# Layer 0's sorted sums with one plain and two weighted spline blocks a direction, the plain blocks copied by ScalarE

## The chip, the cores and the metric

One core of a Trainium2 chip runs the whole program. The metric is the device time of one execution in microseconds (us); the number that counts is the median over several executions. The engines are TensorE (PE, with its weight loads as PEld), VectorE (DVE), ScalarE (ACT), GpSimd (POOL) and SyncE (SP, which only issues DMAs here). Each runs its own instructions in order, and they wait for each other by semaphores.

## The reference

Two layers of a graph network run over 12,500 nodes of 32 features and 400,000 edges, which come sorted by destination. Layer 0 is a spline convolution: every edge has two coordinates in [0, 1]; each gives three hat functions, their products are nine weights, and the message is the source's row times a mix of nine 32 x 32 matrices. Messages are summed by destination, divided by the degree, and a root product, a bias, a residual and a layer norm follow. Layer 1 is relational: four basis matrices, weighted by the edge's type.

```python
p = jnp.clip(pseudo, 0.0, 1.0)
grid = jnp.linspace(0.0, 1.0, KSIZE, dtype=p.dtype)          # KSIZE = 3
dist = jnp.abs(p[:, :, None] - grid[None, None, :])
b = jnp.maximum(1.0 - dist * (KSIZE - 1), 0.0)
basis = jnp.einsum('ea,eb->eab', b[:, 0], b[:, 1])           # then nine in a row
...
messages = jnp.einsum('ek,ei,kio->eo', basis, x[row], weight)
out = jnp.zeros((x.shape[0], weight.shape[2]), dtype=x.dtype).at[col].add(messages)
...
out = out / jnp.maximum(degree, 1.0)[:, None]
out = out + x @ root_w.T + root_b
...
x = _layernorm(x + _L0_gnn_ref(x, edge_attr_2, L0_gnn_weight, L0_gnn_root_w, L0_gnn_root_b, edge_index), axis=-1)
x = _layernorm(x + _L1_gnn_ref(x, L1_gnn_W, L1_gnn_edge_type_weight, src, dst, edge_type_8), axis=-1)
```

For a coordinate in [0, 1] the three hat functions add up to 1. The change uses this.

## The kernel before

The program has three stages: a sorting stage, layer 0 and layer 1. The edges are cut in two parts. The first part (groups 0 to 31 of layer 0's numbering, in blocks of 56 tiles of 128 edges) is the "near" path: its source rows are fetched from memory by POOL, one gather for 128 rows (`gather`, L125), and summed per node (class `Near`, L866 to 1122). The other 90 groups (32 to 121, 2304 edges each) are sorted by source in the first stage, so that their rows can be made on the chip from one-hot products.

For each sorted group, layer 0 does the following (function `layer`, L1145). `take` reads the group's slots (`sl`, L1281) and VectorE makes one-hots from them (`s`, L1293). PE multiplies them with the node rows into one of three PSUM banks (L1303, seven products a bank), and ScalarE moves each bank to its place in `yt` (L1310, 14 moves a group). `use` then goes through the group in three pieces of six chunks of 128 edges. For a piece, PE turns `yt` back into rows `y` in PSUM (L1323, two buffers in one bank). VectorE does three things: `hot_b`, the one-hot of the destination within the group (L1335, 82 places, bf16); `outer`, the rows times the second direction's three spline values (L576, called at L1342, 6 x 3 x 32 = 576 elements); and `spread`, the first direction's three values times the one-hot (L1343, 6 x 3 x 82 = 1476 elements). PE then sums, for each chunk, `outer` (97 columns: three blocks of 32 and a one for the degree) against `spread` (246 columns) into `agg` in PSUM (L1356), over the group's 18 chunks.

The sum of a piece is issued one piece late (`LAG` is 1). `outer` has three buffers (`products`), `spread` three, `hot_b` two. The first direction's spline values `b0_ps` lie in the same PSUM bank as `agg` (L1179): ScalarE writes them once a group (`first_spline`, L1209), and the spread reads them there. The other spline values are made by ScalarE for five groups at a time (`splines`, L1194: six Abs, one Relu).

At a group's end ScalarE copies the sum out of PSUM (`weighing`, L589), and PE multiplies its three blocks, one for each first-direction value, by the matrices in `w0_sb` (L595). `w0_sb` is loaded once, at the start (L203 to 206); its last row holds ones in the degree's column. Work of the near path, of finished nodes (`fin`) and of layer 1's preparation (`mixed`) is put between the pieces. The frame orders instructions by the time it expects them to be ready; in some places the text holds one behind another (`issue_after`).

The last part of the program (from L1489) is a loop over all edges that runs only if the sorting found the data unfit, and it uses `w0_sb` too (L1524).

Of the kernel before, what the change touches and what calls it, by code (L numbers as in the profile page):

```python
# [17 lines left out]
P = 128  # L18
# [4 lines left out]
def kernel(  # L23
# [76 lines left out]
    assert NBL * B == NW  # L100
    assert 8 * NG <= GE // 2 and 1024 <= GE and PER * E == P * N and NGS * CHS * P == E and T1 > 0 and NS * SUB == CH
    assert DUMMY >= N and NG <= P and NTAB // P % 9 == 0 and NCO * CO * CH <= GE
    assert WB * JQ == BT and MAXR % 2 == 0 and 2 * SUB * D + MAXR <= 4 * P and KJ * MAXR + 6 * CH <= 4 * P and NB0 * BT * P <= E and RR <= P
    assert WB * D == P and NTAB >= NW * P and W1 == P
    SRC_UNIT = P * NR
    assert N * SRC_UNIT < 1 << 24
# [95 lines left out]
    nc.sync.dma_start(xr[:TAIL, NW - 1, :], x[(NW - 1) * P:, :])  # L202
    w0_sb = const.tile([P, KJ, D + 1], F32)  # L203
    nc.gpsimd.memset(w0_sb, 0.0)
    nc.vector.memset(w0_sb[KR:KR + 1, :, D:], 1.0)
    nc.sync.dma_start(w0_sb[:KR, :, :D], w0.rearrange("k i o -> (k i) o").rearrange("(j r) o -> r j o", r=KR))
    w1_sb = const.tile([W1, D], F32)
    nc.sync.dma_start(w1_sb, w1.rearrange("b i o -> (b i) o"))
    etw_sb = const.tile([P, NB, NR], F32)
# [362 lines left out]
            nc.vector.memset(t[:, :, W0:], 1.0)  # L572
        return out_

    def outer(t, co, xg, c, k):
        return nc.vector.tensor_tensor(  # L576
            t[:, :c, :k * D].rearrange("p c (k d) -> p c k d", k=k),
            co[:, :, :, None].to_broadcast([P, c, k, D]),
            xg[:, :, None, :].to_broadcast([P, c, k, D]), op=ALU.mult)

# [564 lines left out]
    def layer(which):  # L1145
# [5 lines left out]
        with ExitStack() as stack:  # L1151
# [24 lines left out]
            ys = y_bank[:, :2 * SUB * D].rearrange("p (i c d) -> p i c d", i=2, c=SUB)  # L1176
            sum_bank = ps.tile([P, 4 * P], F32, name="agg")
            if which == 0:
                b0_ps = sum_bank[:, KJ * MAXR:KJ * MAXR + 6 * CH].rearrange(  # L1179
                    "p (i k c) -> p i k c", i=2, k=3)  # L1180
            else:
                col_ps = y_bank[:, 2 * SUB * D:2 * SUB * D + MAXR]
                nc.vector.tensor_copy(col_ps, col[:, :MAXR])
# [10 lines left out]
            def splines(g0):  # L1194
                if g0 <= GF:
                    load_args(g0)
                load_args(g0 + CO)
                args_s = loaded.pop(0)
                b = [cos1.tile([P, 3, CH, CO], F32, name=f"co_b{i}", bufs=2) for i in range(2)]
                for i in range(2):  # L1200
                    for k in range(3):
                        nc.scalar.activation(b[i][:, k], args_s[:, i], AF.Abs,
                                             bias=knot[:, k:k + 1])
                nc.scalar.activation(b[1], b[1], AF.Relu, bias=1.0, scale=-2.0)
                for i in range(CO):
                    co_of[g0 + i] = [t[:, :, :, i] for t in b]
# [107 lines left out]
            def use(g, yt):  # L1314
# [3 lines left out]
                def product(s):  # L1318
                    along(g, s)
                    y = ys[:, (g * NS + s) % 2]  # L1320
                    for c in range(SUB):
                        k = s * SUB + c
                        nc.tensor.matmul(y[:, c, :], yt[:M3, k * P:(k + 1) * P],  # L1323
                                         add3[:M3, :], start=True, stop=True)
                    cs = slice(s * SUB, (s + 1) * SUB)
                    rel = rel_s[:, cs, g, None, :]
                    t = products[(g * NS + s) % NOUT]
                    if which == 0:
                        hot = prods.tile([P, SUB, MAXR], BF16, name="hot_b", bufs=2)
                        spread = prods.tile([P, SUB, 3, MAXR], F32, name="hot")  # L1330
                        b0, b1 = [v[:, cs] for v in co_of[g]]
                    else:
                        hot = spread = prods.tile([P, SUB, MAXR], F32, name="hot")
                    hots[s] = spread
                    nc.vector.tensor_tensor(  # L1335
                        hot.rearrange("p c (m i) -> p c m i", i=2),
                        rel.to_broadcast([P, SUB, MAXR // 2, 2]),
                        (col_ps if which else col_b)[:, None, :]
                        .rearrange("p c (m i) -> p c m i", i=2)
                        .to_broadcast([P, SUB, MAXR // 2, 2]), op=ALU.is_equal)  # L1340
                    if which == 0:
                        last[0] = outer(t, b1, y, SUB, 3)  # L1342
                        nc.vector.tensor_tensor(  # L1343
                            spread, b0[:, :, :, None].to_broadcast([P, SUB, 3, MAXR]),
                            hot[:, :, None, :].to_broadcast([P, SUB, 3, MAXR]), op=ALU.mult)
                    else:
                        last[0] = outer(t, co_of[g][:, cs, :], y, SUB, NB)

# [156 lines left out]
    def weighing_(layer, agg, r):  # L1505
# [15 lines left out]
        def apply():  # L1521
            po = at[0][:, KJ * P:KJ * P + D]
            for j in range(kj):
                nc.tensor.matmul(po, at[1][:, j, :], w1_sb if layer else w0_sb[:KR, j, :D],  # L1524
                                 start=(j == 0), stop=(j == kj - 1))
            nc.scalar.activation(r[:, :D], po, AF.Copy)
            if layer == 0:
# [56 lines left out]
    def from_table(q, tab, width):  # L1584
# [4 lines left out]
                          tab[q0 * P:(q0 + w) * P, :].rearrange("(w p) d -> p w d", p=P))  # L1589
        return t  # L1590

    count = nc.values_load(again[0:1, 0:1], min_val=0, max_val=1)
    with tc.For_i(0, count, 1) as _:
        for t, a, inner in ((src_a, src, 1), (dst_a, dst, 1), (typ_a, edge_type, 1),
                            (attr_a, edge_attr, 2)):
            nc.sync.dma_start(t.rearrange("p (g c) -> p g c", c=CHS * inner),
# [45 lines left out]
```

## Time and profile before

| | |
|---|---|
| median of 6 executions | 6240.28 us (6217.77 to 6282.72) |
| the profiled execution | 6295.12 us, span 6293.3 us |
| mean granted TensorE clock | 0.725 |
| busy over the span | PE 54%, PEld 46%, DVE 48%, ACT 30%, POOL 39% |
| sorting stage | 0 to about 960 us |
| layer 0's sorted groups | about 960 to 3640 us |
| layer 1 | about 3640 to 6293 us |
| DVE spread L1343 | 270 x 1693 ns = 457.2 us |
| DVE outer L576, layer 0 | 270 x 751 ns = 202.7 us |
| DVE hot_b L1335, layer 0 | 270 x 406 ns = 109.7 us |
| PE agg L1356, layer 0 | 3240 records, 847.6 us |
| ACT yt L1310, both layers | 2968 x 384 ns = 1141.0 us |
| POOL gathers of layer 0 L125 | 1505 x 1008 ns |

Busy time is the time in which an engine has an instruction running, whatever it waits for before. "Remote", or an unknown queue, stands where the profile can't tell who ended a wait, and "issue" where the engine waited for nothing that the profile shows. A matmul in f32 appears as two records. Times in this text count from the span's start.

### The profile page before, as it was taken

Reading aid. Unit: us, or ns where it says so; the run is one execution under the profiler, and the core shown is the slowest. Engines: PE = TensorE matmul, PEld = TensorE weight load, DVE = VectorE, ACT = ScalarE, POOL = GpSimd, SP = SyncE. Lnnn points to the kernel's source line nnn. Section 1 sums busy time; section 2 is a strip of 40 time slices with the busy share of each in tenths; the row PEclk is TensorE's granted clock in tenths of the full one; section 3 lists DMA queues with packets and bytes.
Section 4 is the critical chain, followed back from the end, with each engine's and each line's share of the span. In section 5 each row is a group of like instructions: output and inputs, shape, how many; then the busy total and the mean of one; then the engine's idle time right before and its main releaser. Section 6 shows DMA issues by size and latency. Waiting matters only on the chain.

```text
span 6293.3 us, 111686 instructions
## 1 busy us (share of the span) xinstructions
PE 3425.0 (54%) x40923; PEld 2910.0 (46%) x40923; DVE 3046.2 (48%) x5178; ACT 1918.1 (30%) x4768; POOL 2440.5 (39%) x2486
## 2 busy tenths in 40 slices
PE   0221126566556665566556847656555565655558
PEld 0110114455444444455445636555544555555558
DVE  3785776455445554455445625334333334333336
ACT  2664643222222222222222314222222222222224
POOL 5475653333433334433443131333344333334330
PEclk9855557777777777777767868767776677677768
DMA  3000014223222322223222324333333333333333
GB/s 60 8 14 11 13 37 122 84 89 95 80 81 86 95 86 79 86 81 101 81 78 84 117 79 157 110 107 118 111 103 101 103 112 117 108 111 103 104 101 119
DMA packets 266348, 555.44 MB, mean 88 GB/s; under 512 B 84944, under 2 KB 152560, under 8 KB 265300
## 3 DMA queue, kind: packets, MB, share of 16 engines
q1 hardware_dynamic: 184672, 500.96, 24.6%
q0 software_dynamic: 78768, 41.81, 4.9%
q8 instruction: 321, 5.26, 0.3%
q10 hardware_dynamic: 2348, 5.45, 0.3%
q14 instruction: 239, 1.96, 0.1%
HBM read 522.22 MB, written 25.76 MB: 87 GB/s over the span
## 4 chain that ended last, share of the span: by engine, by line
PE 42%; another core or an unknown queue 26%; issue 13%; DVE 11%; ACT 4%; DMA 1%; POOL 1%; ACTq 1%; SPq 0%; DVEq 0%
PE agg L1356 20%; PE bank L1303 13%; PE n_sum L732 3%; PE y L1323 2%; ACT yt L1310 2%; PE n_bank L1052 2%; DVE outer L576 1%; DVE hot L1343 1%; DVE args L387 1%; PE wg L1078 1%; DVE args L386 1%; PE wg L853 1%; PE wg L595 1%; DVE above L379 1%
## 5 line engine op out<-in xcount | busy, mean ns | idle before, releaser
L125 POOL DMA_INDIRECT n_xg<-in_x_dram,n_idx x1505 | 1516.4, 1008 | 1784.5 <-issue 438.5
L1303 PE MATMUL bank<-s,x 128*128 128x108 bf16 (+3 forms) x20776 | 1324.2, 212 | 1410.5 <-issue 962.4
L1310 ACT ACTIVATE yt<-bank x2968 | 1141.0, 384 | 2591.7 <-remote 1273.7
L1303 PEld LDWEIGHTS <-x 128*128 128x128 bf16 x20776 | 1085.7, 105 | 1557.9 <-issue 1489.3
L1356 PE MATMUL agg<-hot,outer 128*128 128x82 f32 (+1 forms) x7632 | 1548.5, 351 | 270.7 <-issue 181.4
L125 POOL DMA_INDIRECT n_xg<-z_dram,near_i x929 | 892.7, 961 | 1723.9 <-PE n_bank L1052 764.5
L1356 PEld LDWEIGHTS agg<-hot,outer 128*128 128x128 f32 (+1 forms) x7632 | 1188.9, 203 | 483.8 <-issue 242.8
L1293 DVE TENSOR_SCALAR s<-sl,row 128x1824 bf16<-128x1824 int16 x848 | 652.6, 772 | 855.4 <-remote 422.9
L1343 DVE TENSOR_TENSOR hot<-agg,hot_b 128x1476 f32<-128x1476 f32 x270 | 457.2, 1693 | 426.7 <-ACT agg_sb L589 134.4
L1335 DVE TENSOR_TENSOR hot<-in_order,y 128x492 f32<-128x492 bf16 x366 | 243.4, 665 | 666.2 <-remote 484.3
L576 DVE TENSOR_TENSOR outer<-co_b,y 128x576 f32<-128x576 f32 x270 | 202.7, 751 | 509.3 <-remote 283.8
L576 DVE TENSOR_TENSOR outer<-co,y 128x768 f32<-128x768 f32 x366 | 346.6, 947 | 0.0
L1323 PE MATMUL y<-add,yt 96*128 96x32 bf16 x3816 | 243.7, 181 | 129.9 <-issue 60.4
L1323 PEld LDWEIGHTS <-yt 96*128 96x128 bf16 x3816 | 203.6, 103 | 158.9 <-issue 152.2
L1052 PE MATMUL n_bank<-n_w,n_xg 128*32 128x72 f32 x3024 | 118.0, 269 | 244.7 <-issue 113.1
L589 ACT ACTIVATE agg_sb<-agg 128x82 f32<-128x82 f32 (+1 forms) x212 | 63.2, 298 | 502.8 <-PE agg L1356 240.2
L237 ACT ACTIVATE in_order<-src,thr 122x2304 bf16<-122x2304 int16 x97 | 213.9, 2205 | 0.5
L1052 PEld LDWEIGHTS n_bank<-n_w,n_xg 128*32 128x32 f32 x3024 | 72.8, 128 | 280.6 <-DVE n_w L1036 117.9
L732 PE MATMUL n_sum<-rows,n_hit 82*128 82x32 f32 (+1 forms) x1056 | 172.6, 287 | 39.3 <-issue 37.9
L732 PE MATMUL n_sum<-n_r,n_hit 112*128 112x33 f32 (+1 forms) x670 | 121.0, 313 | 112.3 <-issue 52.9
L729 DVE TENSOR_SCALAR n_hit<-cols,place_of 82x256 f32<-82x256 f32 (+2 forms) x294 | 94.7, 333 | 171.3 <-remote 68.5
L732 PEld LDWEIGHTS n_sum<-rows,n_hit 82*128 82x128 f32 x1056 | 155.1, 210 | 44.4 <-issue 40.8
(257 smaller groups left out, 2888.1 us busy)
## 6 DMA issues: line engine op xcount, KB each, us to landing
sl<-slots SPq DMA_DIRECT2D x424, 608.0 KB
sl<-slots SPq DMA_DIRECT2D x424, 456.0 KB
n_xg<-in_x_dram,n_idx POOLq DMA_INDIRECT x1505
n_xg<-z_dram,near_i POOLq DMA_INDIRECT x929
hd<-begin_d SPq DMA_DIRECT2D x848, 0.0 KB
z_dram<-n_z SPq DMA_DIRECT2D x49, 256.0 KB
co_d<-co SPq DMA_DIRECT2D x13, 360.0 KB
co<-co_d SPq DMA_DIRECT2D x13, 360.0 KB
```

What stands on the lines that cost most here:

```text
L125: return nc.gpsimd.indirect_dma_start(out=xg, out_offset=None, in_=table, in_offset=bass.IndirectOffsetOnAxis(ap=idx, axis=0))
L237: nc.scalar.activation(t, of[:NG], AF.Sign, bias=bias, scale=scale, accum_out=total)
L576: return nc.vector.tensor_tensor(t[:, :c, :k * D].rearrange("p c (k d) -> p c k d", k=k), co[:, :, :, None].to_broadcast([P, c, k, D]), xg ...
L732: nc.tensor.matmul(total[:, w % WB, :width], hit[:m, i * P:(i + 1) * P], r[:m, :width], start=fresh and i == 0, stop=final and i == len(ws ...
L1052: nc.tensor.matmul(o, self.xg[i][:, at[0], at[1], :], v, start=True, stop=True, tile_position=(0, j * D))
L1293: nc.vector.tensor_scalar(s[:, :n], sl[:, :n], row, None, op0=ALU.is_equal)
L1303: nc.tensor.matmul(bank[:, AHEAD + a:AHEAD + b], parts[:, w * M3:w * M3 + P], s[:, off_[j]:off_[j + 1]], start=(j == 0), stop=(j == B - 1) ...
L1310: moves.append(nc.scalar.activation(yt[:M3, ds(to, LONG)], bank[:M3, ds(place, LONG)], AF.Copy))
L1323: nc.tensor.matmul(y[:, c, :], yt[:M3, k * P:(k + 1) * P], add3[:M3, :], start=True, stop=True)
L1335: nc.vector.tensor_tensor(hot.rearrange("p c (m i) -> p c m i", i=2), rel.to_broadcast([P, SUB, MAXR // 2, 2]), (col_ps if which else col_ ...
L1343: nc.vector.tensor_tensor(spread, b0[:, :, :, None].to_broadcast([P, SUB, 3, MAXR]), hot[:, :, None, :].to_broadcast([P, SUB, 3, MAXR]), o ...
L1356: near.behind = nc.tensor.matmul(agg[0], t[:, c, :], v, start=(k == 0), stop=(k == CH - 1)).ins
```

## The change

The first hat function of each direction is written as one minus the other two. Then the sum over k of b_k W_k becomes W_0 + b_1 (W_1 - W_0) + b_2 (W_2 - W_0), in each direction. So the first of the three blocks of `outer` is the plain rows `y`, and the first of the three blocks of `spread` is the plain one-hot; ScalarE copies both. VectorE multiplies only the other two blocks of each (384 and 984 elements). The splines are made for two values instead of three. The differences of the matrices are taken once, at the start, in `w0_sb`: two more loads of parts of w0 go to `w0_z`, and VectorE subtracts. The degree's one stands in the first block's row alone. The fallback loop keeps the old form, so it gets its own unchanged copy of the matrices (`w0_l`), loaded inside the loop. `agg` keeps its shape.

```diff
--- before.py
+++ after.py
@@ -100,7 +100,7 @@
     assert NBL * B == NW
     assert 8 * NG <= GE // 2 and 1024 <= GE and PER * E == P * N and NGS * CHS * P == E and T1 > 0 and NS * SUB == CH
     assert DUMMY >= N and NG <= P and NTAB // P % 9 == 0 and NCO * CO * CH <= GE
-    assert WB * JQ == BT and MAXR % 2 == 0 and 2 * SUB * D + MAXR <= 4 * P and KJ * MAXR + 6 * CH <= 4 * P and NB0 * BT * P <= E and RR <= P
+    assert WB * JQ == BT and MAXR % 2 == 0 and 2 * SUB * D + MAXR <= 4 * P and KJ * MAXR + 4 * CH <= 4 * P and NB0 * BT * P <= E and RR <= P
     assert WB * D == P and NTAB >= NW * P and W1 == P
     SRC_UNIT = P * NR
     assert N * SRC_UNIT < 1 << 24
@@ -202,8 +202,17 @@
     nc.sync.dma_start(xr[:TAIL, NW - 1, :], x[(NW - 1) * P:, :])
     w0_sb = const.tile([P, KJ, D + 1], F32)
     nc.gpsimd.memset(w0_sb, 0.0)
-    nc.vector.memset(w0_sb[KR:KR + 1, :, D:], 1.0)
+    nc.vector.memset(w0_sb[KR:KR + 1, 0, D:], 1.0)
     nc.sync.dma_start(w0_sb[:KR, :, :D], w0.rearrange("k i o -> (k i) o").rearrange("(j r) o -> r j o", r=KR))
+    w0_z = work.tile([P, P], F32, name="n_xT")[:KR, :KJ * D].rearrange("p (j o) -> p j o", j=KJ)
+    nc.vector.memset(w0_z, 0.0)
+    for k in range(1, 3):
+        nc.sync.dma_start(w0_z[k * D:(k + 1) * D],
+                          w0.rearrange("(j k) i o -> k i j o", k=3)[0])
+    nc.vector.tensor_tensor(w0_sb[:KR, :, :D], w0_sb[:KR, :, :D], w0_z, op=ALU.subtract)
+    for j in range(1, KJ):
+        nc.vector.tensor_tensor(w0_sb[:KR, j, :D], w0_sb[:KR, j, :D], w0_sb[:KR, 0, :D],
+                                op=ALU.subtract)
     w1_sb = const.tile([W1, D], F32)
     nc.sync.dma_start(w1_sb, w1.rearrange("b i o -> (b i) o"))
     etw_sb = const.tile([P, NB, NR], F32)
@@ -572,9 +581,9 @@
             nc.vector.memset(t[:, :, W0:], 1.0)
         return out_
 
-    def outer(t, co, xg, c, k):
+    def outer(t, co, xg, c, k, at=0):
         return nc.vector.tensor_tensor(
-            t[:, :c, :k * D].rearrange("p c (k d) -> p c k d", k=k),
+            t[:, :c, at:at + k * D].rearrange("p c (k d) -> p c k d", k=k),
             co[:, :, :, None].to_broadcast([P, c, k, D]),
             xg[:, :, None, :].to_broadcast([P, c, k, D]), op=ALU.mult)
 
@@ -1176,8 +1185,8 @@
             ys = y_bank[:, :2 * SUB * D].rearrange("p (i c d) -> p i c d", i=2, c=SUB)
             sum_bank = ps.tile([P, 4 * P], F32, name="agg")
             if which == 0:
-                b0_ps = sum_bank[:, KJ * MAXR:KJ * MAXR + 6 * CH].rearrange(
-                    "p (i k c) -> p i k c", i=2, k=3)
+                b0_ps = sum_bank[:, KJ * MAXR:KJ * MAXR + 4 * CH].rearrange(
+                    "p (i k c) -> p i k c", i=2, k=2)
             else:
                 col_ps = y_bank[:, 2 * SUB * D:2 * SUB * D + MAXR]
                 nc.vector.tensor_copy(col_ps, col[:, :MAXR])
@@ -1196,11 +1205,11 @@
                     load_args(g0)
                 load_args(g0 + CO)
                 args_s = loaded.pop(0)
-                b = [cos1.tile([P, 3, CH, CO], F32, name=f"co_b{i}", bufs=2) for i in range(2)]
+                b = [cos1.tile([P, 2, CH, CO], F32, name=f"co_b{i}", bufs=2) for i in range(2)]
                 for i in range(2):
-                    for k in range(3):
+                    for k in range(2):
                         nc.scalar.activation(b[i][:, k], args_s[:, i], AF.Abs,
-                                             bias=knot[:, k:k + 1])
+                                             bias=knot[:, k + 1:k + 2])
                 nc.scalar.activation(b[1], b[1], AF.Relu, bias=1.0, scale=-2.0)
                 for i in range(CO):
                     co_of[g0 + i] = [t[:, :, :, i] for t in b]
@@ -1339,10 +1348,12 @@
                         .rearrange("p c (m i) -> p c m i", i=2)
                         .to_broadcast([P, SUB, MAXR // 2, 2]), op=ALU.is_equal)
                     if which == 0:
-                        last[0] = outer(t, b1, y, SUB, 3)
+                        nc.scalar.activation(t[:, :, :D], y, AF.Copy)
+                        nc.scalar.activation(spread[:, :, 0, :], hot, AF.Copy)
+                        last[0] = outer(t, b1, y, SUB, 2, at=D)
                         nc.vector.tensor_tensor(
-                            spread, b0[:, :, :, None].to_broadcast([P, SUB, 3, MAXR]),
-                            hot[:, :, None, :].to_broadcast([P, SUB, 3, MAXR]), op=ALU.mult)
+                            spread[:, :, 1:, :], b0[:, :, :, None].to_broadcast([P, SUB, 2, MAXR]),
+                            hot[:, :, None, :].to_broadcast([P, SUB, 2, MAXR]), op=ALU.mult)
                     else:
                         last[0] = outer(t, co_of[g][:, cs, :], y, SUB, NB)
 
@@ -1521,7 +1532,7 @@
         def apply():
             po = at[0][:, KJ * P:KJ * P + D]
             for j in range(kj):
-                nc.tensor.matmul(po, at[1][:, j, :], w1_sb if layer else w0_sb[:KR, j, :D],
+                nc.tensor.matmul(po, at[1][:, j, :], w1_sb if layer else w0_l[:, j, :],
                                  start=(j == 0), stop=(j == kj - 1))
             nc.scalar.activation(r[:, :D], po, AF.Copy)
             if layer == 0:
@@ -1589,8 +1600,10 @@
                           tab[q0 * P:(q0 + w) * P, :].rearrange("(w p) d -> p w d", p=P))
         return t
 
+    w0_l = slow.tile([KR, KJ, D], F32, name="l_w0")
     count = nc.values_load(again[0:1, 0:1], min_val=0, max_val=1)
     with tc.For_i(0, count, 1) as _:
+        nc.sync.dma_start(w0_l, w0.rearrange("k i o -> (k i) o").rearrange("(j r) o -> r j o", r=KR))
         for t, a, inner in ((src_a, src, 1), (dst_a, dst, 1), (typ_a, edge_type, 1),
                             (attr_a, edge_attr, 2)):
             nc.sync.dma_start(t.rearrange("p (g c) -> p g c", c=CHS * inner),
```

## The prediction

> **What bounds the kernel now.** I read the shares and slices of the page first, then stretches of 5 us inside layer 0, then the waits of layer 0, then the groups of instructions that the change touches. Layer 0's sorted groups run from 960 to about 3640 us (the first and last spread product, L1343, start at 971.0 and 3628.1 us). The chain of waits names PE for 42%, unknown waits for 26%, and VectorE for only 11%:
>
> ```profile
> PE 42%; another core or an unknown queue 26%; issue 13%; DVE 11%; ACT 4%; DMA 1%; POOL 1%; ACTq 1%; SPq 0%; DVEq 0%
> ```
>
> Stretches of 5 us show why. Columns: time and count of PE, weight load, DVE, ACT, POOL, granted clock, DMA share, GB/s.
>
> ```profile
> 1980.00:1985.00 5.00, 4.99 (x70) 4.27 (x67) 4.71 (x13) 2.22 (x7) 0.83 (x1) 1.00 0.39 141
> ...
> 2000.00:2005.00 5.00, 0.81 (x9) 0.62 (x9) 0.35 (x1) 0.79 (x3) 3.78 (x5) 0.72 0.10 13
> ...
> 2015.00:2020.00 5.00, 0.74 (x3) 0.31 (x3) 0.88 (x2) 0.00 (x0) 3.78 (x5) 0.50 0.07 10
> 2020.00:2025.00 5.00, 0.00 (x0) 0.00 (x0) 0.00 (x0) 0.00 (x0) 3.78 (x5) 0.50 0.09 13
> ...
> 2040.00:2045.00 5.00, 4.73 (x62) 3.92 (x60) 4.90 (x13) 1.69 (x5) 0.00 (x0) 1.00 0.11 40
> ```
>
> Two regimes alternate. POOL issues 28 gathers in a row, 35 us of them; from about 5 us after the first to 6 us after the last, PE, DVE and ACT nearly stand still together, and the clock falls to 0.50. Then all work at full clock until the next gathers. I cut layer 0 between its first and last gather (1008 to 3514 us) into these stretches and summed, the work first:
>
> ```profile
> sum 1198.00, PE 1161.97 PEld 960.48 DVE 1038.87 ACT 518.76 POOL 153.46; mean PE 33.20 PEld 27.44 DVE 29.68 ACT 14.82 POOL 4.38
> ```
>
> and the stalls:
>
> ```profile
> sum 1273.00, PE 353.26 PEld 224.98 DVE 180.83 ACT 108.68 POOL 813.27; mean PE 10.09 PEld 6.43 DVE 5.17 ACT 3.11 POOL 23.24
> ```
>
> In the work, PE is busy 1161.97 of 1198 us, 97%; DVE 87%, ACT 43%. PE's idle time there is 36 us for all reasons together. In the stalls nobody is short of DVE time. After the last gather, from 3520 to 3640 us, PE is busy 114.55 of 120 us: 5.5 us more. So VectorE is the second engine, close behind, and 42 us is all that it can give back, were it to blame for every gap. The waits of layer 0 (1000 to 3600 us; total, times, longest) blame it for less:
>
> ```profile
> ACT yt L1310 <- remote: 670.8, 78, 28.4
> PE bank L1303 <- ACT yt L1310: 213.5, 76, 26.1
> PEld agg L1356 <- DVE hot L1343: 11.3, 28, 1.1
> PE agg L1356 <- DVE hot L1343: 5.4, 13, 1.0
> ```
>
> PE and its weight load wait 16.7 us for the spread, in 41 short waits. PE's wait for ScalarE's move of a bank is larger, but with single waits up to 26.1 us most of it lies in stalls: in five work stretches that I read (160 us in all) it is 0.5, 0, 0.5, 0 and 0 us.
>
> A page speaks against taking 97% busy for a bound: the Trainium skill (Perfetto Trace Analysis, Identifying the Most-Contended Engine) calls matmul busy time a poor measure and prefers the weight load's. By that, PE would be at 960.48/1198 = 80%, with some 240 us of room in the work stretches, and the whole VectorE saving below could come off the time. The trace decides otherwise: in order of time the chain is PE after PE without a gap, with a piece's twelve agg products at 2.55 us:
>
> ```profile
> 2115.41 0.57 PE bank L1303 x14
> 2115.98 0.42 PE n_sum L732 x4
> 2116.40 2.55 PE agg L1356 x12
> 2118.95 0.84 PE bank L1303 x21
> ```
>
> **The change, part by part.** A piece is six chunks; there are 90 groups x 3 = 270 pieces. The rows:
>
> ```profile
> L1343 DVE TENSOR_TENSOR hot<-agg,hot_b 128x1476 f32<-128x1476 f32 x270 | 457.2, 1693 | 426.7 <-ACT agg_sb L589 134.4 <-remote 97.7 <-ACT agg L1209 97.7
> L576 DVE TENSOR_TENSOR outer<-co_b,y 128x576 f32<-128x576 f32 x270 | 202.7, 751 | 509.3 <-remote 283.8 <-PE agg L1356 67.7 <-issue 66.1
> ```
>
> ```profile
> L1310 ACT ACTIVATE yt<-bank x1255 | 481.8, 384 | 1132.2 <-remote 670.8 <-PE bank L1303 303.1 <-issue 42.2
> L1202 ACT ACTIVATE co_b<-co_a,knot 128x90 f32<-128x90 f32 x114 | 38.1, 361 | 8.3 <-DVE outer L576 7.0 <-issue 0.8
> L589 ACT ACTIVATE agg_sb<-agg 97x246 f32<-97x246 f32 x90 | 33.9, 377 | 341.4 <-PE agg L1356 147.4 <-remote 115.3 <-issue 52.4
> L1060 ACT ACTIVATE n_agg<-n_bank 128x504 f32<-128x504 f32 x39 | 22.9, 588 | 9.2 <-PE n_bank L1052 4.9 <-PE y L1323 1.6 <-PE bank L1303 0.4
> ```
>
> *VectorE.* The outer goes from 576 to 384 elements. Layer 1's outer has 768 at 947 ns, so 192 elements are 196 ns: 751 - 196 = 555. The spread goes from 1476 to 984; L1036's two forms (576 at 749 ns, 864 at 1050) give 1.045 ns an element: 1693 - 492 x 1.045 = 1179. Together 0.71 us a piece, 270 x 0.71 = 192 us of VectorE. The 210 pieces in the work stretches (the spread is busy 355.5 us there, over 1.693) take it from 87% to 74%. On the path: the spread reads the bank that agg is summed in, so it stands between two runs of agg; a group's end is agg 2.55 + sum's copy 0.38 + next splines 0.27 + spread 1.69, some 4.9 us with handoffs still to add, against 5.5 us of PE work a piece (1161.97 / 210). That ring turns faster than PE. Gain: at least 0, at most the 42 us of all gaps; the named waits are 16.7, partly the same time seen twice, so I take half: -8 us. PE hides the rest.
>
> *ScalarE.* L589's forms (246 at 377 ns, layer 1's 82 at 240) give 0.835 ns an element. The copy of y, 192 elements: 377 - 54 x 0.835 = 332 ns. The copy of the plain one-hot, 492: 377 + 246 x 0.835 = 582 (L1060 agrees: 588 for 504). 0.914 us a piece, 247 us. Splines lose a third: 38 of 114 Abs at 361 ns, 13.7 us, and 3 us of the shorter Relus. Net +230 us, in the work stretches 518.8 + 210 x 0.914 - 13 = 698 of 1198: ScalarE from 43% to 58%. It is not the bound, but it is in order, and behind the two copies stand the yt moves that free PE's three banks, and the sum's copy. The y copy waits for PE's y, the other for VectorE's one-hot; before, ScalarE waited for neither. The one-hot is usually made a few us ahead (2037.65 us, its spread at 2043.14). Price: at least 0 (every copy falls into ScalarE's 42% of idle time), at most 247 us (each copy keeps PE waiting for its full length). Between: a queue's wait goes with busy/idle, 0.43/0.57 = 0.76 before, 0.58/0.42 = 1.39 after, 1.8 times. The five stretches give 1 us in 160, 8 us over 1318; were all 42 us of gaps ScalarE's, 42. Growth by 0.8: 7 to 34. I take +17, nearer to what the waits name.
>
> *PE* does the same products: agg keeps 97 x 246. It now waits for two writers of each operand and, for y's buffer, two readers; both are a piece (5.5 us) ahead, so nothing. If the copies lag by more than a piece, it is the slower rival.
>
> *Stalls.* 29 pieces' spreads (48.8 us / 1.693) fall into them. More handoffs could cost that progress: at most 29 x 5.5 = 160 us, at least 0; handoffs in a stall end together with it, so I take 0.
>
> *Start.* Two more loads on SP's queue beside w0's (0.33 us each; w1, the type weights, block0 and the first edge loads move 0.7 us back), and a memset and three subtractions on VectorE (about 0.28 each by L830's 286 ns). VectorE is in order there and the sort behind it; L830 already stands 2.9 us for a load. 0 to +5, taken +3. The load in the fallback loop isn't run (nothing of that loop is in the trace).
>
> Sum: -8 + 17 + 0 + 3 = +12 us, 6295 to 6307 in the profiled execution. That run stands 0.9% above the median of 6240, so the median becomes 6252.
>
> **Rivals.** *Slower: ScalarE's queue becomes PE's wait.* In each piece the y copy or the one-hot copy stands until its source is there, with yt moves behind it, and PE finds its banks full. It decides once a move is later than the three banks' worth of products (21 in 0.85 us) plus what other work PE has ready. At 0.3 us a piece, a third of the copies' length: 270 x 0.3 = 81, 6321 us. For it: PE bank already waits for yt, and both new waits sit ahead of it. Against: PE runs 2.55 us of agg between its runs of banks, longer than two moves (0.77) and both copies.
>
> *Faster: the ring of agg and spread, not PE alone, sets the work's pace.* The 4.9 us above is near 5.5; groups that miss it show as the 41 waits. All 42 us of gaps go: 6240 - 42 + 3 = 6201. For it: DVE at 87% in order. Against: only 16.7 of 42 us name the spread.
>
> *Does not do what it says:* the copies and the shorter products write interleaved parts of one tile; if they are kept in order against each other, VectorE's spread stands behind ScalarE's copy and part of the saving is waiting. 26% of idle VectorE time covers that: near 6260.
>
> **How the numbers follow.** Forecast 0.42 (6252, itself 6225 to 6285), third rival 0.08, slower rival 0.3, faster 0.2. A measurement here can tell about 0.5%, 31 us. Faster by more: nearly the whole faster case and a little of the forecast, 0.22; slower: the slower case and some of the forecast's top, 0.36; the rest 0.42. Range 6195 (all gaps gone) to 6335 (0.35 us a piece).
>
> **What would show it.** Right: outer near 555 ns, spread near 1180, copies near 330 and 580; work stretches with PE still near 97% and DVE near 74%; waits of PE for the spread almost gone, those for yt up by some 10 to 20 us outside stalls; stalls unchanged at 35 us each. Wrong: PE under 95% there with waits for yt or for the copies (slower rival), shorter work stretches with PE at 99% (faster rival), or a different number or length of stalls, which I have taken as fixed.

## The result, and the profile after

The change made the kernel slower: median 6287.04 us (6262.82 to 6325.79, 24 runs) against 6245.72 us (6211.56 to 6311.98, 50 runs) for the kernel before, measured beside it. The ratio is 1.0066, 95% interval 1.005 to 1.0083. That is +41 us, where the forecast said +12. The profiled execution took 6317.76 us, its span is 6316.0 us (6293.3 before). In the code after, the lines have moved: the bank product is L1312, `yt` L1319, `y` L1332, the two new copies L1351 and L1352, the spread L1354, the outer L585, agg L1367, the sum's copy L598.

The chain of waits after, which read PE 42%, DVE 11% and 26% unknown before:

```profile
PE 43%; another core or an unknown queue 30%; issue 11%; DVE 9%; ACT 5%; DMA 1%; ACTq 1%; POOL 0%; SPq 0%; DVEq 0%
```

VectorE lost two points of the chain, and the unknown waits gained four; these stand for waits in the stalls, as below. Next the page's groups, the size of each edited instruction (columns: count, busy us and mean ns of one, idle time before it and what ended that):

```profile
L1354 DVE TENSOR_TENSOR hot<-agg,hot_b 128x984 f32<-128x984 f32 x270 | 318.9, 1181 | 497.3 <-ACT agg_sb L598 169.9
...
L1352 ACT ACTIVATE hot<-hot_b 128x492 f32<-128x492 bf16 x270 | 163.7, 606 | 221.7 <-PE agg L1367 107.1
L585 DVE TENSOR_TENSOR outer<-co_b,y 128x384 f32<-128x384 f32 x270 | 148.3, 549 | 186.7 <-ACT outer L1351 109.2
```

and, from the groups kept apart by shape, the copy of y:

```profile
L1351 ACT ACTIVATE outer<-y 128x192 f32<-128x192 f32 x270 | 89.1, 330 | 296.0 <-remote 196.4 <-PE y L1332 68.9 <-PE agg L1367 13.4
```

The spread takes 1181 ns and the outer 549, the copies 606 and 330. The parts have the sizes that the forecast gave them, within 5%. VectorE's busy time fell from 3046 to 2886 us, ScalarE's rose from 1918 to 2087, PE's is the same (3425 and 3419). The last idle column of the outer already shows something new: VectorE stands 109.2 us for ScalarE's copy, in a tile of which the two write different parts.

The stages, each from one profile. Layer 0, from its first one-hot `s` to its last agg product, before and after (columns: window, its length, busy us and count of PE, weight load, DVE, ACT and POOL, granted clock, DMA share, GB/s):

```profile
954.70:3635.10 2680.40, 1684.04 (x17902) 1321.78 (x17902) 1376.61 (x2565) 703.88 (x2063) 993.67 (x1018) 0.76 0.30 90
...
941.00:3661.40 2720.40, 1676.21 (x17902) 1319.70 (x17902) 1214.11 (x2562) 872.93 (x2561) 986.32 (x1018) 0.76 0.30 89
```

The sorting stage ahead of it fell from 954.7 to 941.0 us, layer 0 rose from 2680.4 to 2720.4 (+40), the rest fell from 2658 to 2655. So the loss lies in layer 0. The same cut as before, between layer 0's first and last gather, into 35 work stretches and 35 stalls; the work after:

```profile
sum 1240.00, PE 1200.82 PEld 987.98 DVE 932.59 ACT 659.48 POOL 148.70; mean PE 34.31 PEld 28.23 DVE 26.65 ACT 18.84 POOL 4.25
```

and the stalls after:

```profile
sum 1271.00, PE 308.81 PEld 195.62 DVE 151.41 ACT 121.08 POOL 810.54; mean PE 8.82 PEld 5.59 DVE 4.33 ACT 3.46 POOL 23.16
```

The stalls are as long as before (1271 us, 1273 before). But PE was busy for 308.81 us in them, where it had been for 353.26: 44 us less. What it didn't do there was left for the stretches between, where PE is still the bound at 1200.82/1240 = 97%, as before: PE's busy time there rose by 39 us, and the stretches by 42. PE's idle time in them is 39 us, 36 before.

The 44 us and the 39 us are not the same work, though. PE runs slower in a stall (mean granted clock 0.58, against 0.93 in the stretches), so 44 us there are worth less outside. Counted in pieces, by the spread's busy time over the length of one, the stalls held 48.8/1.693 = 28.8 pieces before and 28.0/1.181 = 23.7 after: five fewer, at some 5.5 us each 28 us. Counted by PE's own products, each kind at what one took in the stretches of before, it is some 22 us. Both are estimates. The rest of the 39 us is then the same products taking longer, which runs 9 and 10 show without stalls.

The waits of layer 0 (total us, times, longest) show the handoffs concerned:

```profile
ACT yt L1319 <- remote: 397.4, 57, 23.3
...
PE bank L1312 <- ACT yt L1319: 287.0, 66, 23.4
...
ACT outer L1351 <- remote: 196.4, 22, 22.0
...
DVE outer L585 <- ACT outer L1351: 108.6, 39, 26.4
...
ACT hot L1352 <- remote: 84.7, 5, 22.8
```

ScalarE's unknown waits ahead of a yt move fell from 670.8 to 397.4 us, and the copies ahead of it in the queue now have 196.4 + 84.7 = 281 us of such waits: the stall finds ScalarE at a copy instead. PE's wait for the yt moves rose from 213.5 to 287.0 us, and the two copies and the outer behind them have waits that did not exist before. Single waits of 20 us and more, in a kernel where a piece takes 5.5, are waits in a stall. What such a wait is can be read in the trace of before: in the stall at 2134 us PE's last agg product of a group ended at 2138.9 us, and ScalarE's copy of that sum started at 2164.45, with two gathers of the row still to come. The sum was done; that word of it came 26 us late is read from this, for the profile names no releaser (it puts 23.5 us of the wait under "issue"). PE, too, stood in this stall before products for which the profile shows no wait, six times, up to 1.2 us, so late handoffs are not all of a stall.

### The profile page after: what moved, and what is told of

Read it like the earlier page. It is cut to its first block, busy times and chain, and to the rows that moved or that the text cites. A ratio compares the mean times of both kernels' runs of the same rounds, so it can differ in the third digit from the quotient of the medians.

```text
span 6316.0 us, 112437 instructions
## 1 busy us (share of the span) xinstructions
PE 3418.6 (54%) x40923; PEld 2907.4 (46%) x40923; DVE 2885.8 (46%) x5182; ACT 2086.8 (33%) x5270; POOL 2440.6 (39%) x2486
## 4 chain that ended last, share of the span: by engine, by line
PE 43%; another core or an unknown queue 30%; issue 11%; DVE 9%; ACT 5%; DMA 1%; ACTq 1%; POOL 0%; SPq 0%; DVEq 0%
PE agg L1367 20%; PE bank L1312 13%; PE n_sum L741 3%; ACT yt L1319 2%; PE y L1332 2%; PE n_bank L1061 2%; DVE outer L585 1%; ACT in_order L246 1%; PE wg L1087 1%; PE wg L862 1%; DVE args L396 1%; PE wg L604 1%; DVE args L395 1%; DVE args_d L395 1%
## 5 line engine op out<-in xcount | busy, mean ns | idle before, releaser
L1312 PE MATMUL bank<-s,x 128*128 128x108 bf16 (+3 forms) x20776 | 1317.4, 212 | 1436.7 <-issue 930.2
L1312 PEld LDWEIGHTS <-x 128*128 128x128 bf16 x20776 | 1092.0, 105 | 1632.2 <-issue 1550.2
L1319 ACT ACTIVATE yt<-bank x2968 | 1136.5, 383 | 2005.6 <-remote 1073.3
L1367 PE MATMUL agg<-hot,outer 128*128 128x82 f32 (+1 forms) x7632 | 1539.5, 348 | 244.7 <-issue 161.0
L1367 PEld LDWEIGHTS agg<-hot,outer 128*128 128x128 f32 (+1 forms) x7632 | 1171.8, 201 | 410.2 <-issue 192.4
L1354 DVE TENSOR_TENSOR hot<-agg,hot_b 128x984 f32<-128x984 f32 x270 | 318.9, 1181 | 497.3 <-ACT agg_sb L598 169.9
L585 DVE TENSOR_TENSOR outer<-co,y 128x768 f32<-128x768 f32 x366 | 346.6, 947 | 0.0
L1332 PE MATMUL y<-add,yt 96*128 96x32 bf16 x3816 | 246.8, 181 | 136.6 <-issue 74.7
L1332 PEld LDWEIGHTS <-yt 96*128 96x128 bf16 x3816 | 210.6, 104 | 157.6 <-issue 152.7
L1061 PE MATMUL n_bank<-n_w,n_xg 128*32 128x72 f32 x3024 | 148.5, 266 | 220.5 <-issue 138.3
L1352 ACT ACTIVATE hot<-hot_b 128x492 f32<-128x492 bf16 x270 | 163.7, 606 | 221.7 <-PE agg L1367 107.1
L585 DVE TENSOR_TENSOR outer<-co_b,y 128x384 f32<-128x384 f32 x270 | 148.3, 549 | 186.7 <-ACT outer L1351 109.2
L598 ACT ACTIVATE agg_sb<-agg 128x82 f32<-128x82 f32 (+1 forms) x212 | 63.0, 297 | 401.8 <-PE agg L1367 194.3
L607 ACT ACTIVATE rows<-wg 82x32 f32<-82x32 f32 (+1 forms) x212 | 41.0, 194 | 446.9 <-remote 386.7
```

The source lines that it names most:

```text
L585: return nc.vector.tensor_tensor(t[:, :c, at:at + k * D].rearrange("p c (k d) -> p c k d", k=k), co[:, :, :, None].to_broadcast([P, c, k, D]),
L1061: nc.tensor.matmul(o, self.xg[i][:, at[0], at[1], :], v, start=True, stop=True, tile_position=(0, j * D))
L1312: nc.tensor.matmul(bank[:, AHEAD + a:AHEAD + b], parts[:, w * M3:w * M3 + P], s[:, off_[j]:off_[j + 1]], start=(j == 0), stop=(j == B - 1) ...
L1319: moves.append(nc.scalar.activation(yt[:M3, ds(to, LONG)], bank[:M3, ds(place, LONG)], AF.Copy))
L1332: nc.tensor.matmul(y[:, c, :], yt[:M3, k * P:(k + 1) * P], add3[:M3, :], start=True, stop=True)
L1354: nc.vector.tensor_tensor(spread[:, :, 1:, :], b0[:, :, :, None].to_broadcast([P, SUB, 2, MAXR]), hot[:, :, None, :].to_broadcast([P, SUB, ...
```

## The experiments

Three theories. A: the change adds handoffs between engines (PE to ScalarE for the copy of y, ScalarE to VectorE in a shared tile), and in a stall each handoff can come tens of us late, so less gets done per stall. B: ScalarE's time alone is the cost; its queue makes the yt moves late. C: any edit makes the frame order the instructions anew, and the difference is luck of the order. That C has a footing shows in the order of PE's products in layer 0. Counted as runs of products of one kind that follow each other, the same 17902 records come in 1633 runs before, in 1975 in the change, in 1720 with the idle copies below, which leave PE's work untouched, and in 1636 in the tiny control.

The twelve runs went to three chips, and this shaped what they could say. On the first (runs 1 to 4) and the second (5 to 8) the same kernel before takes 3705.19 us (3691.55 to 3720.02, 35 runs) and 3702.19 us (3690.47 to 3716.84, 31 runs): the gathers are issued at the same pace, but no engine stands still in them. On the third (9 to 12) it stalls and takes 6263.66 us (6208.47 to 6295.65, 23 runs). The first four expectations were written before that was known. So runs 1 to 8 tell what each part costs without stalls, and runs 9 to 12 what the stalls add. The change without stalls, layer 0 of run 5 (columns as above):

```profile
900.00:2200.00 1300.00, 1278.85 (x15845) 1057.81 (x15845) 1066.26 (x2262) 767.53 (x2274) 1011.96 (x946) 1.00 0.53 162
```

PE is busy 98% of it at full clock, with POOL busy 78% with gathers.

**1. The change without the copies.** The plain blocks are filled with ones once, so VectorE's saving is there alone.

```diff
-                        spread = prods.tile([P, SUB, 3, MAXR], F32, name="hot")
+                        spread = spreads[(g * NS + s) % NOUT]
...
-                        nc.scalar.activation(t[:, :, :D], y, AF.Copy)
-                        nc.scalar.activation(spread[:, :, 0, :], hot, AF.Copy)
```

> The change without ScalarE's two copies: the plain blocks of both products are filled with ones once, so the sums of layer 0 are not the reference's; VectorE's shorter products, the shorter splines and the loads at the start stay. Theory A (handoffs: the copies give ScalarE two more waits a piece, which stand in the gather stalls with the yt moves behind them, so less work gets done in a stall): 0 to -20 us against before, PE busy in the stalls back near 350 us. Theory B (ScalarE's time alone makes the yt moves late): the same, 0 to -20. Theory C (any edit of layer 0 reorders the instructions, and the 41 us are that): anything from -40 to +40, most likely still +20 to +40.

Measured: 3694.6 us, ratio 0.9975 (0.9958 to 0.9993). VectorE's saving comes out at about 10 us without stalls, near the -8 of the forecast; run 2, which saves nothing, came out 8 us faster too, so this says little more than that it is small. B and A both allowed it; the loss of 20 to 40 us that C held most likely is not there.

**2. Before, with two copies a piece that nobody reads** (300 and 384 elements).

```diff
+                idle = outs.tile([P, 384], mybir.dt.uint8, name="idle")
...
+                        nc.scalar.activation(idle[:, :300], block0.rearrange("p k j d -> p (k j d)")[:, :300], AF.Copy)
+                        nc.scalar.activation(idle, block0.rearrange("p k j d -> p (k j d)")[:, :384], AF.Copy)
```

> The kernel before, with two ScalarE copies added a piece that wait for no other engine and that nobody reads (300 and 384 elements, about 0.9 us a piece, as long as the change's two). Theory A: +0 to +12 us, for the time alone is not the loss. Theory B: +35 to +60 us, the whole loss of the change and its missing VectorE saving. Theory C: anything from -40 to +40.

Measured: 3696.84 us, 0.998 (0.9964 to 0.9997). ScalarE's time costs nothing here; theory B, which said +35 to +60, falls for a chip without stalls. And a kernel with nothing but more to do came out 8 us faster: some 0.2% can come from the order alone, as theory C has it.

**3. The copy of y alone**: the outer takes two values, the spread three as before (with its splines and weights).

```diff
-                        nc.scalar.activation(spread[:, :, 0, :], hot, AF.Copy)
...
-                            spread[:, :, 1:, :], b0[:, :, :, None].to_broadcast([P, SUB, 2, MAXR]),
-                            hot[:, :, None, :].to_broadcast([P, SUB, 2, MAXR]), op=ALU.mult)
+                            spread, b0[:, :, :, None].to_broadcast([P, SUB, 3, MAXR]),
+                            hot[:, :, None, :].to_broadcast([P, SUB, 3, MAXR]), op=ALU.mult)
```

> One part of the change: the rows' product takes two values and ScalarE copies the plain rows (which wait for PE's y); the spread keeps its three values. Theory A: +20 to +35 us, for the wait for PE's y is the one that a stall stretches. Theory B: +10 to +15 us (0.33 of 0.91 us of ScalarE a piece). Theory C: anything from -40 to +40.

Measured: 3686.4 us, 0.9956 (0.994 to 0.9972).

**4. The one-hot's copy alone**: the spread takes two values, the outer three as before (likewise).

```diff
-                        nc.scalar.activation(t[:, :, :D], y, AF.Copy)
...
-                        last[0] = outer(t, b1, y, SUB, 2, at=D)
+                        last[0] = outer(t, b1, y, SUB, 3)
```

> The other part alone: the spread takes two values and ScalarE copies the plain one-hot (which waits for VectorE and for a free buffer); the rows' product keeps its three values. Theory A: +5 to +20 us. Theory B: +20 to +30 us (0.58 of 0.91 us a piece, less the bigger VectorE saving). Theory C: anything from -40 to +40.

Measured: 3695.34 us, 0.9974 (0.9958 to 0.9989). Each half alone is as good without stalls as all savings without any copy (run 1), so within the 0.2% that an order can make neither copy is a cost there. The losses that A and B gave for runs 3 and 4 did not come; those of A were written for a chip with stalls.

**5. The change itself**, on the second chip, beside runs 6 to 8.

> The change itself, beside the kernel before on one chip. In the four runs so far the chip showed no stalls at the gathers (the kernel before takes 3705 us there). Theory A (the change loses in the gather stalls alone): where the gathers stall the engines, +0.4 to +0.9% again; where they do not, -0.3 to -0.8%, the two parts' -0.26 and -0.44% together or a little less. Theory B (ScalarE's time): +0.3% or more on either. Theory C (reordering): within 0.3% of before on a chip without stalls, with no relation to the parts.

Measured: 3691.68 us, 0.9976 (0.9962 to 0.999). The kernel that is 0.66% slower on a chip with stalls is 0.24% faster on one without, a little less than the 0.3 to 0.8% of theory A. Two of its waits in layer 0:

```profile
DVE outer L585 <- ACT outer L1351: 16.5, 26, 2.0
...
PE bank L1312 <- ACT yt L1319: 12.0, 33, 1.1
```

Where these were 108.6 and 287.0 us, with single waits above 23 us, they are 16.5 and 12.0, none above 2.0. The same instructions wait on the same partners; only the stalls make the waits long.

**6. VectorE's products ahead of ScalarE's copies in the text.** If the two are kept in order, ScalarE now waits and VectorE doesn't.

```diff
-                        nc.scalar.activation(t[:, :, :D], y, AF.Copy)
-                        nc.scalar.activation(spread[:, :, 0, :], hot, AF.Copy)
                         last[0] = outer(t, b1, y, SUB, 2, at=D)
...
+                        nc.scalar.activation(t[:, :, :D], y, AF.Copy)
+                        nc.scalar.activation(spread[:, :, 0, :], hot, AF.Copy)
```

> The change with the two ScalarE copies put behind VectorE's two products in the text, so that where the four writes of the two operands are kept in order, ScalarE stands behind VectorE and not VectorE behind ScalarE. If VectorE's wait for the copies (109 us of waits of the rows' product in the profile after) is part of the loss: 0.2 to 0.5% better than the change in the same call. If ScalarE's queue is what matters: the same as the change or up to 0.3% worse, because ScalarE now waits longer in front of the yt moves.

Measured: 3683.03 us, 0.9956 (0.9935 to 0.9976). The wait turned round with the text:

```profile
ACT outer L1355 <- DVE outer L585: 86.4, 130, 1.9
```

So writers of different, interleaved parts of one tile are kept in order, in the order of the text. Whether this order is better than the change's is not settled: the intervals overlap.

**7. The comparison writes the one-hot straight into the spread's first block**; the copy of the one-hot is gone.

```diff
-                        hot = prods.tile([P, SUB, MAXR], BF16, name="hot_b", bufs=2)
                         spread = prods.tile([P, SUB, 3, MAXR], F32, name="hot")
+                        hot = spread[:, :, 0, :]
...
-                        nc.scalar.activation(spread[:, :, 0, :], hot, AF.Copy)
```

> The change without the one-hot copy: VectorE's comparison writes the plain one-hot in f32 straight into its block of the spread, and the spread's product reads it there; ScalarE copies the plain rows only. VectorE pays up to 0.26 us more a piece (layer 1's comparison to f32 takes 665 ns, the bf16 one 406), 70 us in all, ScalarE saves 0.6 us a piece. Theory A: without stalls the same as the change within 0.2%; with stalls better than it by 0.1 to 0.4% (one handoff fewer). Theory B: better than the change by 0.3% or more on either.

Measured: 3692.17 us, 0.9984 (0.9969 to 0.9998). No better than with the copy.

**8. Both copies twice.**

```diff
                         nc.scalar.activation(spread[:, :, 0, :], hot, AF.Copy)
+                        nc.scalar.activation(t[:, :, :D], y, AF.Copy)
+                        nc.scalar.activation(spread[:, :, 0, :], hot, AF.Copy)
```

> The change with each of ScalarE's two copies done twice. ScalarE has 250 us more and no new kind of wait. Theory A: without stalls +0 to +0.3% over the change, with stalls +0.1 to +0.4%. Theory B: the loss doubles, +0.6% or more over the change on either. It also tells how much room ScalarE has left.

Measured: 3692.88 us, 0.9974 (0.9959 to 0.9989), against 0.9976 for one set. Twice the suspected cost costs nothing: theory B falls a second time, again on a chip without stalls.

**9 and 10. Before and the change with layer 0's gathers cut**, on the chip with stalls. Each unit keeps one of its gathers, and all of its near products read that one.

```diff
-            return b * BT + t < self.T
+            return self.which == 1 and b * BT + t < self.T
```

> The kernel before with one gather a unit of the near path of layer 0 where there were 28, and every near product reading that one buffer: layer 0's near sums are not the reference's, PE has the same products to do. It shows what the gathers themselves cost. Where gathers stall the engines: 1200 to 1700 us faster (some 36 stalls of 35 us in layer 0 and those of the first stage). Where they do not: 0 to 60 us faster, since PE is busy 98% of layer 0 beside them.

> The change with the same cut of the gathers. Theory A (the change loses in the gather stalls): against the same cut of the kernel before it is 0 to 0.5% faster, on either kind of chip. Theory B (ScalarE's time in the work stretches): 0.3% slower or more. Theory C (order): within 0.4% of it, either way.

Measured: before 4789.49 us (4782.77 to 4799.83, 6 runs), the change 4805.75 us (4801.6 to 4822.12, 5 runs); as ratios to the full kernel before, 0.7657 (0.7633 to 0.768) and 0.7682 (0.7657 to 0.7707). Layer 0 of before with its gathers cut, and of the change (windows as for the full kernels):

```profile
680.10:2145.00 1464.90, 1428.30 (x17902) 1186.51 (x17902) 1366.20 (x2565) 699.67 (x2063) 52.09 (x46) 0.99 0.46 153
...
684.10:2162.50 1478.40, 1446.03 (x17902) 1195.50 (x17902) 1201.00 (x2562) 862.89 (x2560) 52.41 (x46) 1.00 0.46 153
```

POOL has 52 us of work, the clock is full, PE 98% busy: the stalls of layer 0 are gone, and layer 0 takes 1464.9 and 1478.4 us, where the full kernel before takes 2680.4. What is left of the change's loss is 4805.75 - 4789.49 = 16 us, with ranges that don't overlap. Against the 41 us with the stalls, about 25 us go with them. That is a difference of medians, and the 41 were not measured beside these runs.

The 0.34% that are left go against theory A, which had the change 0 to 0.5% faster here. By the number alone they fit B (0.3% slower or more) and C (within 0.4%). The rows decide between these two. In layer 0 PE's idle time went down, from 36.6 to 32.4 us, and so did its wait for the yt moves, here from 750 to 2060 us:

```profile
PE bank L1303 <- ACT yt L1310: 14.8, 46, 0.7
...
PE bank L1312 <- ACT yt L1319: 10.7, 28, 1.4
```

So nothing here waits longer for ScalarE. Layer 0 is 13.5 us longer because PE is busy 17.7 us longer with the same 17902 records. The place is the near path's products `n_bank`, whose busy time, part of it shared with products beside them, is, before and in the change:

```profile
680.10:2145.00 1464.90, 62.48 (x2184) 39.69 (x2184) 0.99 0.46 153
...
684.10:2162.50 1478.40, 86.35 (x2184) 49.37 (x2184) 1.00 0.46 153
```

One of them takes no longer by itself (256 and 257 ns), but they overlap less: by the trace they come in 130 groups before and in 211 in the change, 77 of these a single product of two records. The order of PE's, VectorE's and ScalarE's instructions in layer 0, by the names of what they write and read, is the same in run 9 as in the full kernel before, and in run 10 the same as in the change and in run 5. In the full kernels the same row goes from 73.9 to 99.8 us, and in run 5 it is 86.4. So these 16 us are a cost of the order that the frame chose for the change, not of ScalarE's time.

**11. The change with VectorE making both copies.**

```diff
-                        nc.scalar.activation(t[:, :, :D], y, AF.Copy)
-                        nc.scalar.activation(spread[:, :, 0, :], hot, AF.Copy)
+                        nc.vector.tensor_copy(t[:, :, :D], y)
+                        nc.vector.tensor_copy(spread[:, :, 0, :], hot)
```

> The change with VectorE making the two plain copies, so that the sums are the change's and ScalarE has no new work. VectorE pays two copies (192 elements from PSUM, 492 from bf16), some 0.2 to 0.6 us a piece, less than the 0.71 us that the shorter products save. Theory A: where gathers stall, no slower than before (+-0.3%), 0.4 to 0.7% better than the change; elsewhere within 0.2% of the change. Theory B: better than the change by 0.2% or more on either. Theory C: within 0.4% of before, either way.

Measured: 6259.79 us (6217.18 to 6301.29), 0.9999 (0.9966 to 1.0031). The interval lies below that of the change (1.005 to 1.0083). Its copies, from the groups kept apart by shape:

```profile
L1352 DVE CAST hot<-hot_b 128x492 f32<-128x492 bf16 x270 | 112.8, 418 | 58.4 <-remote 38.8 <-PE agg L1367 18.4
...
L1351 DVE COPY outer<-y 128x192 f32<-128x192 f32 x270 | 96.3, 357 | 659.1 <-remote 446.5 <-PE y L1332 144.1 <-PE bank L1312 58.4
```

They take 112.8 + 96.3 = 209 us, and the shorter products had saved 192: VectorE has as much to do as before. Combined weights, interleaved blocks and copies are all there; in the text only the engine of the copies differs. Its stalls:

```profile
sum 1277.00, PE 334.46 PEld 221.08 DVE 189.34 ACT 110.16 POOL 820.50; mean PE 9.56 PEld 6.32 DVE 5.41 ACT 3.15 POOL 23.44
```

PE is busy 334.46 us in them, so of the 44 us that the change loses there more than half is back; counted in spreads, 36.1/1.181 = 30.5 pieces, all of it. But run 11 has an order of its own as well: its near products come in 128 groups and take 73.0 us, as before. All three theories had forecast about this number, so the time alone doesn't choose between A and C.

**12. Before, with one copy of eight elements a group**: what a new instruction alone does.

```diff
+                idle = outs.tile([P, 8], F32, name="idle")
...
+                        if s == 0:
+                            nc.scalar.activation(idle, block0[:, 0, 0, :8], AF.Copy)
```

> The kernel before with one ScalarE copy of 8 elements a group (90 in all, some 0.18 us each) that waits for nothing and is read by nobody: a control for what a new order of the instructions alone does. Theory C: a difference of 0.15% or more from before, of either sign. Theories A and B: within 0.1%.

Measured: 6246.75 us (6209.97 to 6287.0), 0.9985 (0.9953 to 1.0018): no difference that can be told. Its stalls, for comparison:

```profile
sum 1273.00, PE 347.62 PEld 220.03 DVE 180.70 ACT 109.56 POOL 813.29; mean PE 9.93 PEld 6.29 DVE 5.16 ACT 3.13 POOL 23.24
```

347.62 us of PE's work, near the 353.26 of before. Four profiles on chips with stalls thus give 353, 348, 334 and 309 us (28.8, 31.0, 30.5 and 23.7 pieces), and layer 0 takes 2680.4, 2688.1, 2667.9 and 2720.4 us in them: the first three, within 0.5% of each other in the time of the whole kernel, stand apart from the change.

## Why the prediction was right, and where it was not

The direction and the range held (slower, 6287 within 6195 to 6335). The likeliest time, 6252, was 35 us too low. By the steps of the sum:

- **The sizes of the parts** were right: outer 549 ns (555 forecast), spread 1181 (1179), copies 330 and 606 (332 and 582). PE at 97% in the work stretches and VectorE at 932.59/1240 = 75% came as forecast (97 and 74); ScalarE reached 53%, below the forecast 58%: 659 us where 698 were forecast, in stretches that grew to 1240.
- **VectorE, -8 us.** Run 1 gives about -10 without stalls, within what an order alone can make. PE is the bound, and hides the rest of 192 us. The waits of PE and its weight load for the spread, 16.7 us before between 1000 and 3600 us, are gone there (over the whole run 31.5 us became 5.0), as forecast.
- **ScalarE, +17 us.** This term is not borne out. Idle copies (run 2) and doubled copies (run 8) cost nothing without stalls. With the gathers cut the change does cost 16 us, but PE waits less for the yt moves there, 10.7 us against 14.8, and in the work stretches of the full kernels it waits as long as before (15.5 us against 15.6), where the prediction's sign was 10 to 20 us more. The number is met by another cause.
- **PE, "the same products ... so nothing".** The products are the same, but not PE's time for them: 17.7 us more with the gathers cut (runs 9 and 10), as the new order breaks up the groups of near products. The prediction had no term for the order.
- **Stalls, +0 us.** The prediction saw that "More handoffs could cost that progress: at most 29 x 5.5 = 160 us, at least 0", and then took 0 because "handoffs in a stall end together with it". The stalls' length is unchanged, as forecast, but less gets done in them: five pieces of 29, worth 22 to 28 us by the estimates above, which PE had to do in stretches where it was the bound. About 25 of the 41 us go away when the stalls do (runs 9 and 10).
- **Start, +3 us.** The sorting stage was 14 us shorter in the one profile after. One pair of profiles doesn't tell it from chance: the same stage takes 931.1 us in the tiny control, whose start is that of before. It wasn't tested.
- **The slower rival** named the yt moves, but put its price on every piece, with PE short of banks. PE's share in the work stretches did not fall, so this is not how it went; the long waits for yt are waits in stalls.
- **The third rival** was given 0.08 and is right as far as the order goes: VectorE's outer stands behind ScalarE's copy, 108.6 us with stalls and 16.5 without, and run 6 turned it round. That this is the handoff which costs the progress in the stalls is argued, not shown: run 6 was not tried on a chip with stalls.
- **The faster rival** needed PE to wait for the ring of agg and spread. The 42 us of gaps did not go: 39 us are left.

That the change came out slower, as forecast, is thus in part luck: the term that made the sum positive, ScalarE's queue, is the one that the runs don't find, and the loss came by two ways that the sum held at nothing.

Shown: the loss lies in layer 0. Some 16 us of it are there without the gathers, as PE's own time for the same products in another order; some 25 us more need the stalls, in which fewer pieces get done. A kernel with the copies on VectorE loses neither. Not settled: whether the 25 us are theory A or C. The change reorders nearly everything, and what happens to be at hand when a stall begins is part of what can be done in it; run 11 has the same edits but for the engine, yet an order of its own. Nor is it settled why the whole kernel is 16 us slower on the third chip with its gathers cut and 11 us faster on the second with them: no profile of before was taken on the second. No variant beat the kernel before where it stalls. Without stalls the best were runs 3 and 6, both 0.9956, of which neither was tried with stalls.

## What to carry to other kernels

A step that moves to an idle engine is not free by that engine's idle time. It can make the frame reorder the work of the engine that is the bound: compare that engine's busy time for the same products before and after, here 17.7 us, and not only its waits. It also adds handoffs, which have to be priced in the part of the run where waits are longest, here the stalls; that they are what cost the 25 us is likely, not shown. Before shortening an engine's work, look at which engine is busy in the stretch concerned: with PE at 97%, 192 us less for VectorE was worth about 10 at most. A gain or loss below one per cent should be seen on more than one chip, and beside a control that only disturbs the order, before it is believed.

## What was not expected of the hardware

The same program takes 6264 us on one chip and 3702 or 3705 us on two others. The difference is what happens while POOL issues its gathers. The next lines are from the change's profile on a chip with stalls, inside a run of gathers; columns as for run 5:

```profile
2010.00:2015.00 5.00, 0.48 (x2) 0.21 (x2) 1.21 (x5) 0.00 (x0) 3.78 (x5) 0.50 0.39 98
2015.00:2020.00 5.00, 0.63 (x2) 0.52 (x2) 0.00 (x0) 0.00 (x0) 3.78 (x5) 0.50 0.11 13
```

and the same kernel on the second chip, in gathers too:

```profile
1105.00:1110.00 5.00, 5.00 (x62) 4.37 (x62) 4.75 (x12) 2.75 (x8) 3.78 (x5) 1.00 0.51 154
1110.00:1115.00 5.00, 5.00 (x73) 4.06 (x71) 4.43 (x10) 2.83 (x8) 4.07 (x4) 1.00 0.46 138
```

POOL is equally busy, 3.78 us in five gathers of each 5 us, and a gather's median length is 944 and 947 ns on the two kinds of chip. Beside it PE does 0.6 us of work on the one and 5.0 on the other, at clock 0.50 and 1.00. In the stall of before that was read above, the profile shows no late code: the fetches of instructions next to it, at 2134 and 2173 us, ended in about 1 us, and none fell into it. Why the engines stand still in one chip's gathers and not in another's stays open. Cutting the gathers in layer 0 removed 1215 us of its 2680 on the chip that stalls (run 9), some thirty times the difference that this study was about.
